# A causal convolution folded into its projection's weights, and the gates' products moved one stage later

## The chip, the cores and the metric

The kernel runs on one core of one Trainium2 chip. The metric is device time in microseconds (us) from the start to the end of one execution; the kernel before was run three times, and its median is given. A core has five engines that work side by side: TensorE multiplies matrices (PE in the profile, PEld for its weight loads), VectorE (DVE) and ScalarE (ACT) work element by element, GpSimd (POOL) too, and SyncE (SP) issues the DMAs here. Each takes its instructions in order.

## The reference

The input x is 16 images of 256 channels and 32x32 points. Layer 0 is x + attention block(group norm(x)). Layer 1, with which the change deals, is a Mamba-like layer: for each image, with L = 1024 tokens,

```python
xs = group_norm(x) as tokens + (rel_h + rel_w)              # (L, 256)
ctx = sigmoid(conv1d(xs, gate_w, 3 taps, pad 1) + gate_b)   # the gates, (L, 256)
u, z = split(xs @ in_proj_w.T)                              # (L, 512) each
uc[l] = conv_b + sum over t in 0..3 of conv_w[:, t] * u[l - 3 + t]   # each channel alone, causal
u = silu(uc)
dt, Bm, Cm = split(u @ x_proj_w.T)                          # 16, 64, 64
delta = softplus(dt @ dt_proj_w.T + dt_proj_b)              # (L, 512)
h[l] = exp(delta[l] * A) * h[l - 1] + delta[l] * u[l] * Bm[l]   # 512 x 64 states
y[l] = h[l] . Cm[l] + u[l] * D
out = x + ((y * silu(z)) @ out_proj_w.T) * ctx
```

All of it is fp32, but for delta's pieces, which are held as three bf16 parts.

## The kernel before, in words

**The scan.** Images ("batches", b) are done one after the other. The state recurrence of a batch is cut into 256 units (b, t, k, q, i): 2 halves of the tokens, 4 blocks of 128 channels, 4 quarters, 8 pairs of channels. A unit handles 2 x 64 states on 128 partitions and 512 tokens, twice (e = 0, 1). `load` fetches delta*u spread over the partitions (tile dub, L832), `inputs` multiplies it by B on GpSimd (L842), `decay` multiplies a selection matrix by delta's pieces on TensorE (L851) and takes exp on ScalarE (L854), `scan` runs the recurrence on VectorE (L864), and `outputs` sums h*C over the states on TensorE, in bursts of 64 passes (L901), copies (L909) and turns (L913).

**The side work.** Beside batch b's scans, a Python generator issues what batch b+1 needs, and what batch b-1 has still to do: `first_norm`, `gate_and_store` (of b-1), `attention_layer`, and `scan_inputs`, in this order. Each `yield` names the cost of the step just issued. The main loop deals the steps over the units at an even rate:

```python
total = steps * len(parts)        # steps: sum of the yields of one preparation
...
total += GATE
...
rate, due = total / (UNITS - AHEAD - 3), 0.0
```

so that a change of any yield changes how many units each stage is spread over. In a unit n the order is load(n+6), inputs(n+4), scan(n), decay(n+2), then the side steps that have come due, then a step of `outputs`. On TensorE, ScalarE, VectorE and GpSimd the program order is kept as written; SyncE's DMAs may be placed otherwise. Batch 0's preparation runs alone, ahead of the first scan, and beside the last batch only `gate_and_store` runs.

**The stages of `scan_inputs`.** In order: group norm (into xp, with room for one zero on each side), the position added, the z stage (L580, L585, L569), the u stage, the x stage (L667, L671), softplus (L686 to L733). In the u stage `project(d, hf)` multiplies a half (512 tokens) of block d by its weights, two products of 128 rows each (L601), copies it to `up` (L606) and starts `u` with the last tap and the bias (L607). `tap(d, t)` adds one of the other three taps on VectorE over 1024 tokens (L615). Then tanh (L652) and u = (tanh + 1) * u (L655) make the silu. `gate(o, hf, q)` makes a quarter of the gates' block o: six products of 256 columns and one for the bias (L630, L634), and after every second one a tanh (L636). Gates are interleaved with the taps. Each step of a u block costs 1.6, four of them, and the first two projections 1 each.

**Buffers.** Tiles of 1024 columns come from the pool `wide` (10 buffers), weights of a stage from one tile of 4672 columns, matrix products from the pool mm (2 banks of PSUM) beside the scan; the pool accp is one bank, used by attention. `decay` has 4 banks, two units' worth.

Of the kernel before, what the change touches and what calls it, by code (L numbers as in the profile page):

```python
# [11 lines left out]
F32 = mybir.dt.float32  # L12
BF16 = mybir.dt.bfloat16
AF = mybir.ActivationFunctionType
ALU = mybir.AluOpType
# [4 lines left out]
P = 128  # L20
C = 256
KC = C // P
L = 1024
HL = 512
# [4 lines left out]
DI = 512  # L29
ND = DI // P  # L30
NS = 64
RANK = 16
CONV = 4
# [19 lines left out]
def attention_then_scan_kernel(  # L53
# [18 lines left out]
    nc = tc.nc  # L72
    B = x.shape[0]

    def pool(name, bufs, **kw):
        return ctx.enter_context(tc.tile_pool(name=name, bufs=bufs, **kw))

    const = pool("const", 1)
    wts = pool("wts", 1)
    wide = pool("wide", 10)  # L80
    half = pool("half", 4)
    ptp = pool("ptp", 4)
    small = pool("small", 2)
# [4 lines left out]
    dram1 = pool("dram1", 1, space=DRAM)  # L88
# [9 lines left out]
    def psum(name, dims=P):  # L98
        src = mm if beside["scan"] else next(alone)
        return src.tile([P, HL], F32, name=name, tag="mm" if src is mm else "a")[:dims]  # L100

    def work(name, n=L):
        return wide.tile([P, L + 2 + CONV], F32, name=name, tag="wide")[:, :n]

    def hwork(name):
        return half.tile([P, HL], F32, name=name, tag="half")

    def hs(h):
        return ts(h, HL)
# [67 lines left out]
    t = work("ones_s")[:1]  # L177
# [9 lines left out]
        nc.sync.dma_start(rel[ts(k, P), :], t)  # L187


    def weights(*specs):  # L190
        w = wts.tile([P, 4672], F32, name="w", tag="w")
        at, views, fetches = 0, [], []
        for src, k in specs:
            n = src.shape[-1]
            if k == 0:
                v = w[: src.shape[0], at : at + n]
                at += n
            else:
                v = w[:, at : at + k * n].rearrange("p (k e) -> p k e", k=k)
                src = src.rearrange("(k p) e -> p k e", p=P)  # L200
                at += k * n
            views.append(v)
            fetches.append(partial(nc.sync.dma_start, v, src))
        return views, fetches
# [102 lines left out]
    def fetch(to, src, k):  # L307
        t = work("xs")
        nc.sync.dma_start(t, src[ts(k, P), :])  # L309
        to.append(t)  # L310
# [226 lines left out]
    def scan_inputs(b):  # L537
        st = state[b]
        (win_s, wg_s, wx_s, wdt_s), bring = weights(
            (w_in, KC), (w_gate.rearrange("c t o -> c (t o)"), KC), (w_x, ND), (w_dt, 0)  # L540
        )
        wg_s = wg_s.rearrange("p k (t o) -> p k t o", t=3)
        xs = st.pop("xs")
        xp = [work("xp", L + 2) for _ in range(KC)]
        body = [t[:, 1 : L + 1] for t in xp]
        for t in xp:
            nc.vector.memset(t[:, 0:1], 0.0)
            nc.vector.memset(t[:, L + 1 : L + 2], 0.0)
        rels = []
        yield from along(  # L550
            group_norm(xs, body),
            [partial(nc.sync.dma_start, st["xr"][ts(k, P), :], xs[k]) for k in range(KC)]
# [14 lines left out]
        def finish_z():  # L567
            for d, hf, z, t, ps in ready:
                nc.vector.scalar_tensor_tensor(z[:, hs(hf)], t, 1.0, ps, ALU.add, ALU.mult)  # L569
                if hf == 1:  # L570
                    nc.sync.dma_start(zs[ts(d, P), :], z)
            ready.clear()

        for d in range(ND):
            z = work("z")
            for hf in range(2):
                finish_z()
                ps = psum("z_ps")
                for k in range(KC):
                    nc.tensor.matmul(  # L580
                        ps, win_s[:, k, ds(DI + d * P, P)], body[k][:, hs(hf)],
                        start=(k == 0), stop=(k == KC - 1),
                    )
                t = hwork("z_t")
                nc.scalar.activation(t, ps, AF.Tanh, scale=0.5)  # L585
                ready.append((d, hf, z, t, ps))
                yield 1
        del z, t, ps

        us, ups = [], []  # L590
        ud = dram.tile([DI, L], F32, name="ud", tag="ud")
        gs = dram.tile([C, L], F32, name="gs", tag="gs")

        def project(d, hf):
            if hf == 0:
                ups.append(work("up", L + CONV - 1))
                nc.vector.memset(ups[d][:, : CONV - 1], 0.0)
                us.append(work("u"))
            ps = psum("u_ps")
            for k in range(KC):  # L600
                nc.tensor.matmul(  # L601
                    ps, win_s[:, k, ts(d, P)], body[k][:, hs(hf)],
                    start=(k == 0), stop=(k == KC - 1),
                )
            last = d * CONV + CONV - 1
            nc.scalar.copy(ups[d][:, ds(CONV - 1 + hf * HL, HL)], ps)  # L606
            nc.scalar.activation(  # L607
                us[d][:, hs(hf)], ps, AF.Identity,
                bias=cbh[:, d : d + 1], scale=cwh[:, last : last + 1],
            )  # L610

        def tap(d, t):
            i = d * CONV + t
            u = us[d]
            nc.vector.scalar_tensor_tensor(  # L615
                u, ups[d][:, t : t + L], cwh[:, i : i + 1], u, ALU.mult, ALU.add
            )

        gates = {}

        def gate(o, hf, q):
            if (hf, q) == (0, 0):
                gates["g"] = work("g")
            if q == 0:
                gates["ps"] = psum("g_ps")
            g, ps = gates["g"], gates["ps"]
            first = o * HL + hf * 2 + q
            for i in range(3 * KC):
                k, t = divmod(i, 3)
                nc.tensor.matmul(  # L630
                    ps[:, ts(q, C)], xp[k][:, ds(first + t, P, 4)], wg_s[:, k, t, :],
                    start=(i == 0), stop=False,
                )
            nc.tensor.matmul(ps[:, ts(q, C)], one_row, gate_b, start=False, stop=True)  # L634
            if q == 1:
                nc.scalar.activation(g[:, hs(hf)], ps, AF.Tanh, scale=0.5)  # L636
                if hf == 1:
                    nc.sync.dma_start(gs[ts(o, P), :], g)

        finish_z()  # L640
        project(0, 0)
        yield 1
        project(0, 1)
        yield 1
        for d in range(ND):
            for t in range(2):
                tap(d, t)
                if d + 1 < ND:
                    project(d + 1, t)
                yield 1.6  # L650
            tap(d, 2)
            nc.scalar.activation(ups[d][:, :L], us[d], AF.Tanh)  # L652
            gate(d // 2, d % 2, 0)
            yield 1.6
            nc.vector.scalar_tensor_tensor(us[d], ups[d][:, :L], 1.0, us[d], ALU.add, ALU.mult)  # L655
            ups[d] = None
            nc.sync.dma_start(ud[ts(d, P), :], us[d])
            gate(d // 2, d % 2, 1)
            yield 1.6
        gates.clear()  # L660
        del xp, body
        dt, bc = work("dt"), work("bc")
        for hf in range(2):
            for dst, lo, n in ((dt, 0, RANK), (bc, RANK, 2 * NS)):
# [38 lines left out]
        yield 1  # L703
        for d in range(ND):
            items = [more(d, *items[0]), begin(d, 1)]
            yield 1
            items[1] = more(d, *items[1])
            rest(*items[0])
            yield 1.4
            rest(*items[1])  # L710
            for ps, e, s in items:
                nc.scalar.activation(s, s, AF.Ln)
            yield 1.7
            pc = [ptp.tile([P, L], BF16, name="pc", tag="pt") for _ in range(3)]
            for hf, (ps, e, s) in enumerate(items):
                nc.vector.tensor_tensor(ps, s, ps, ALU.subtract)
                nc.scalar.copy(pc[0][:, hs(hf)], ps)
            yield 1.4
            du = work("du")
            for hf, (ps, e, s) in enumerate(items):  # L720
                nc.vector.tensor_tensor(du[:, hs(hf)], us[d][:, hs(hf)], ps, ALU.mult)
            nc.sync.dma_start(duv[d], du.rearrange("d (t c) -> d t c", t=NT))
            yield 1.4
            for hf, (ps, e, s) in enumerate(items):
                nc.vector.tensor_tensor(ps, ps, pc[0][:, hs(hf)], ALU.subtract)
                nc.scalar.copy(pc[1][:, hs(hf)], ps)
            yield 1.4
            for hf, (ps, e, s) in enumerate(items):
                nc.vector.tensor_tensor(pc[2][:, hs(hf)], ps, pc[1][:, hs(hf)], ALU.subtract)
            items, ps, e, s = [], None, None, None  # L730
            for p in range(3):
                for e in range(2):
                    nc.sync.dma_start(dpv[d, p, e], pc[p][e:P:2])  # L733
            if d + 1 < ND:
                items = [begin(d + 1, 0)]
            yield 1.4
        st.update(zs=zs, gs=gs, ud=ud, rows=rows, dps=dps, dus=dus)
        st["ys"] = dram.tile([DI, L], F32, name="ys", tag="ys")
        yield 1
# [321 lines left out]
```

## Time and profile before

| what | us |
|---|---|
| median of 3 runs (13815.34 to 13842.49) | 13833.62 |
| the profiled execution, whole | 13784.86 |
| its span, first to last instruction | 13782.7 |
| start of the first scan | 392.9 |
| one batch of 256 units, seven batches in | 849.4 |
| last batch (only `gate_and_store` beside it) | 676.7 |
| VectorE busy, all | 12135.5 |
| TensorE busy, all | 11113.2 |
| GpSimd busy, all | 10477.2 |
| taps L615, all 192 | 300.9 |

Durations below come from the profiled execution, and comparisons of whole times are made from the median. A group's line reads: source line, engine, operation, output<-inputs, shapes, count | busy us, mean ns of one | idle time of the engine ahead of it, and what ended that. The granted TensorE clock (PEclk) is a share of full speed.

### The profile page before, as it was taken

To read this page: it belongs to the slowest core of one execution; us is meant where nothing else is said; L and a number is where in the kernel's file an instruction comes from. 1 tells how busy PE (TensorE), PEld (TensorE's weight loads), DVE (VectorE), ACT (ScalarE), POOL (GpSimd) and SP (SyncE) were. 2 spreads that over 40 slices of the span, in tenths; PEclk is the share of its full clock that TensorE was granted. 3 is DMA by queue.
4 is the path that set the end of the run, shared out by engine and by line. 5 is a ranking of instruction groups with operands and counts; after the bars stand their busy time and mean duration, and the time that the engine had idled before them with its cause. 6 is when DMAs were issued, how large, how long until landed. Compare 5 with 4: busy or idle time off the path is not lost. (4 is left out here: it accounts for less than half of the span.)

```text
span 13782.7 us, 435036 instructions
## 1 busy us (share of the span) xinstructions
PE 11113.2 (81%) x185744; PEld 5728.7 (42%) x185744; DVE 12135.5 (88%) x11699; ACT 8088.7 (59%) x14245; POOL 10477.2 (76%) x8214
## 2 busy tenths in 40 slices
PE   7787878878787787978879788797887978878767
PEld 3344444444444444444444444444444444434434
DVE  3898898898898889888898888889888898888898
ACT  3666665656655565655656655566555655556644
POOL 0787777777787777777777787777777777777788
PEclk8686767867777686876767777677776776867767
DMA  1566566565665656556565565656656565565666
GB/s 55 196 207 230 187 214 208 201 222 196 211 207 199 218 201 223 194 199 218 197 231 186 197 226 191 232 185 202 219 191 230 187 214 205 194 228 187 209 219 223
DMA packets 964174, 2804.18 MB, mean 203 GB/s; under 512 B 138162, under 2 KB 285747, under 8 KB 962228
## 3 DMA queue, kind: packets, MB, share of 16 engines
q1 hardware_dynamic: 962228, 2776.34, 58.8%
q8 instruction: 1452, 23.79, 0.7%
q14 instruction: 494, 4.05, 0.1%
HBM read 2514.18 MB, written 261.62 MB: 201 GB/s over the span
## 5 line engine op out<-in xcount | busy, mean ns | idle before, releaser
L842 POOL TENSOR_TENSOR dub<-dub,bt 128x512 f32<-128x512 f32 x8192 | 10422.4, 1307 | 3254.5 <-DMA dub<-dus 2878.4
L854 ACT ACTIVATE a<-a,acol 128x512 f32<-128x512 f32 x8192 | 5064.9, 660 | 3728.2 <-PE a L851 3689.1
L864 DVE TENSOR_TENSOR_SCAN h<-a,last,dub 128x512 f32<-128x512 f32 x4096 | 4932.9, 1261 | 227.0 <-POOL dub L842 128.8
L864 DVE TENSOR_TENSOR_SCAN h<-a,dub 128x512 f32<-128x512 f32 x4096 | 4700.9, 1201 | 276.7 <-POOL dub L842 186.6
L851 PE MATMUL a<-pieces,pick 48*128 48x512 bf16 x8192 | 2914.9, 480 | 2103.1 <-DVE h L864 2037.8
L901 PEld LDWEIGHTS yb<-h,cd 128*32 128x32 f32 x131072 | 2677.2, 140 | 2166.2 <-issue 1847.3
L901 PE MATMUL yb<-h,cd 128*32 128x64 f32 x131072 | 3090.5, 265 | 160.9 <-DVE yb L891 115.9
L851 PEld LDWEIGHTS <-pick 48*128 48x128 bf16 x8192 | 498.0, 96 | 2507.4 <-issue 2293.2
L408 PE MATMUL s_ps<-ka,qa 32*128 32x512 f32 x2048 | 1115.7, 1009 | 23.2 <-DVE mx L399 15.2
L399 DVE TENSOR_REDUCE mx<-s_ps 128x1 f32<-128x512 f32 x1024 | 654.9, 678 | 279.0 <-PE s_ps L408 278.2
L913 PEld LDWEIGHTS yb<-turn,y 128*16 128x16 f32 x32768 | 418.9, 120 | 960.3 <-ACT y L909 484.6
L909 ACT COPY y<-yb 128x256 f32<-128x256 f32 x1024 | 383.4, 374 | 693.6 <-PE yb L901 688.3
L913 PE MATMUL yb<-turn,y 128*16 128x32 f32 x32768 | 555.2, 216 | 193.8 <-ACT y L909 173.0
L444 PE MATMUL st_ps<-qa,ka 33*128 33x512 f32 x2048 | 590.2, 613 | 25.9 <-ACT pt L452 25.5
L432 PE MATMUL av<-pt,vv 128*64 128x512 f32 x2048 | 572.7, 635 | 4.3 <-ACT sums L390 3.3
L452 ACT ACTIVATE pt<-st_ps 128x512 f32<-128x512 f32 x1024 | 558.9, 609 | 28.8 <-PE st_ps L444 28.4
L408 PEld LDWEIGHTS s_ps<-ka,qa 32*128 32x128 f32 x2048 | 345.4, 274 | 402.3 <-DVE mx L399 221.4
L630 PE MATMUL g_ps<-w,xp 128*128 128x256 f32 x1536 | 475.2, 468 | 0.0
L630 PEld LDWEIGHTS g_ps<-w,xp 128*128 128x128 f32 x1536 | 401.9, 329 | 137.6 <-issue 92.6
L789 PE MATMUL m_ps<-w,xs 128*128 128x256 f32 x1024 | 316.7, 459 | 10.9 <-DVE xs L764 10.9
L921 ACT COPY yo<-yb 128x256 f32<-128x256 f32 x512 | 193.1, 377 | 222.2 <-PE yb L913 219.7
L615 DVE SCALAR_TENSOR_TENSOR u<-up,cwh,u 128x1024 f32<-128x1024 f32 x192 | 300.9, 1567 | 23.8 <-ACT u L607 23.6
(135 smaller groups left out, 7593.8 us busy)
## 6 DMA issues: line engine op xcount, KB each, us to landing
dub<-dus SPq DMA_DIRECT2D x4096, 512.0 KB
dps<-pc SPq DMA_DIRECT2D x384, 128.0 KB
pieces<-dps SPq DMA_DIRECT2D x1024, 48.0 KB
xs<-in_x_dram SPq DMA_DIRECT2D x64, 512.0 KB
xs<-kept SPq DMA_DIRECT2D x64, 512.0 KB
zs<-z SPq DMA_DIRECT2D x64, 512.0 KB
ud<-u SPq DMA_DIRECT2D x64, 512.0 KB
dus<-du SPq DMA_DIRECT2D x64, 512.0 KB
```

Source lines behind the costliest of these rows:

```text
L399: nc.vector.tensor_reduce(mx[:, e, c, hf : hf + 1], s, AX.X, ALU.max)
L408: nc.tensor.matmul(s, qa[r, ts(c, P)], ka[r, hs(hf)], start=True, stop=True)
L432: nc.tensor.matmul(av[ts(e, 2 * DH)], vv[j // (NJ // 2)][:, j % (NJ // 2), 2 * pair + e, :], pts[e], start=(j == 0), stop=(j == NJ - 1),)
L444: nc.tensor.matmul(s, ka[r, ts(j, P)], qa[r, hs(hf)], start=True, stop=True)
L452: nc.scalar.activation(pt, s, AF.Exp)
L630: nc.tensor.matmul(ps[:, ts(q, C)], xp[k][:, ds(first + t, P, 4)], wg_s[:, k, t, :], start=(i == 0), stop=False,)
L842: nc.gpsimd.tensor_tensor(v, v, blocks[b, t]["bt"], ALU.mult)
L851: nc.tensor.matmul(a, w, pieces[r], start=True, stop=True)
L854: nc.scalar.activation(a, a, AF.Exp, scale=acol[:, at : at + 1])
L864: nc.vector.tensor_tensor_scan(now["h", q % 2][:, 2 * i + e, :], decays[n][e], loaded[n][:, e, :], first, ALU.mult, ALU.add,)
L901: nc.tensor.matmul(yb[ts(g, 32), ts(s, 64)], cd[:, at // 16, ts(c, 32)], hbuf[:, :, at : at + 4], start=(c == 0), stop=(c == 3),)
L913: nc.tensor.matmul(out4[32 * s : 32 * s + 16, half, e], y2[:, 64 * s + e : 64 * s + 64 : 4], turn[:, e], start=True, stop=True,)
```

## The change

The convolution's taps go into the weights: conv_w[e, t] * in_proj_w[e, c] is a weight matrix for each tap t, and u of a block is the sum over 2 halves of the channels and 4 taps of one product each, with the tokens shifted by t, all summed in PSUM. These weights are computed once, ahead of everything, on GpSimd, and kept in DRAM (wcv, 512 KB for each of 4 blocks); each batch fetches them, block by block. xp has three zeros ahead and one behind. ScalarE takes tanh of the sum into SBUF and adds the bias in place, and VectorE makes the silu in halves, one step later (`finish_u`). The calls of `gate` move from the u stage into softplus, two for each d, with their sums in accp's bank. Only z's half of w_in is fetched among the weights. The yields change: the u stage's sum goes from 27.6 to 17.2, softplus' from 39.8 to 42.6. The diff, cut to its core:

```diff
-    wide = pool("wide", 10)
+    wide = pool("wide", 11)
...
+    wcv = dram1.tile([ND * P, KC * CONV * P], F32, name="wcv", tag="wcv")
+    taps = dram1.tile([ND * CONV, P], F32, name="taps", tag="taps")
+    ps = psum("taps_ps", ND * CONV)[:, :P]
+    nc.tensor.matmul(ps, cwh, ident, start=True, stop=True)
+    t = work("taps_s", P)[: ND * CONV]
+    nc.scalar.copy(t, ps)
+    nc.sync.dma_start(taps, t)
+    wu = work("wu").rearrange("p (k e) -> p k e", k=KC)
+    nc.sync.dma_start(wu, w_in[:, :DI].rearrange("(k p) e -> p k e", p=P))
+    for d in range(ND):
+        if d % 2 == 0:
+            row = work("row")
+            nc.sync.dma_start(
+                row,
+                taps[ds(d * CONV, 2 * CONV)].rearrange("i e -> (i e)").partition_broadcast(P),
+            )
+        t = work("wcs").rearrange("p (k t e) -> p k t e", k=KC, t=CONV)
+        for k in range(KC):
+            nc.gpsimd.tensor_tensor(
+                t[:, k], row[:, ts(d % 2, CONV * P)].rearrange("p (t e) -> p t e", t=CONV),
+                wu[:, k, ts(d, P)].unsqueeze(1).to_broadcast([P, CONV, P]), ALU.mult,
+            )
+        nc.sync.dma_start(wcv[ts(d, P), :], t.rearrange("p k t e -> p (k t e)"))
...
-            (w_in, KC), (w_gate.rearrange("c t o -> c (t o)"), KC), (w_x, ND), (w_dt, 0)
+            (w_in[:, DI:], KC), (w_gate.rearrange("c t o -> c (t o)"), KC), (w_x, ND), (w_dt, 0)
...
-        xp = [work("xp", L + 2) for _ in range(KC)]
-        body = [t[:, 1 : L + 1] for t in xp]
+        xp = [work("xp", L + CONV) for _ in range(KC)]
+        body = [t[:, CONV - 1 : CONV - 1 + L] for t in xp]
...
+        def finish_u():
+            for d, hf, t, ps in ready:
+                nc.vector.scalar_tensor_tensor(us[d][:, hs(hf)], t, 1.0, ps, ALU.add, ALU.mult)
+                if hf == 1:
+                    nc.sync.dma_start(ud[ts(d, P), :], us[d])
+            ready.clear()
...
         def project(d, hf):
             if hf == 0:
-                ups.append(work("up", L + CONV - 1))
-                nc.vector.memset(ups[d][:, : CONV - 1], 0.0)
                 us.append(work("u"))
+            w = wcs[d].rearrange("p (k t e) -> p k t e", k=KC, t=CONV)
             ps = psum("u_ps")
-            for k in range(KC):
+            for i in range(KC * CONV):
+                k, t = divmod(i, CONV)
                 nc.tensor.matmul(
-                    ps, win_s[:, k, ts(d, P)], body[k][:, hs(hf)],
-                    start=(k == 0), stop=(k == KC - 1),
+                    ps, w[:, k, t], xp[k][:, ds(hf * HL + t, HL)],
+                    start=(i == 0), stop=(i == KC * CONV - 1),
                 )
-            last = d * CONV + CONV - 1
-            nc.scalar.copy(ups[d][:, ds(CONV - 1 + hf * HL, HL)], ps)
-            nc.scalar.activation(
-                us[d][:, hs(hf)], ps, AF.Identity,
-                bias=cbh[:, d : d + 1], scale=cwh[:, last : last + 1],
-            )
-
-        def tap(d, t):
-            i = d * CONV + t
-            u = us[d]
-            nc.vector.scalar_tensor_tensor(
-                u, ups[d][:, t : t + L], cwh[:, i : i + 1], u, ALU.mult, ALU.add
-            )
+            t = hwork("u_t")
+            nc.scalar.activation(t, ps, AF.Tanh, bias=cbh[:, d : d + 1])
+            nc.scalar.activation(ps, ps, AF.Identity, bias=cbh[:, d : d + 1])
+            ready.append((d, hf, t, ps))
...
-                gates["ps"] = psum("g_ps")
+                gates["ps"] = accp.tile([P, HL], F32, name="g_ps", tag="av")
...
+        fetch(wcs, wcv, 0)
         finish_z()
-        project(0, 0)
-        yield 1
-        project(0, 1)
         yield 1
         for d in range(ND):
-            for t in range(2):
-                tap(d, t)
-                if d + 1 < ND:
-                    project(d + 1, t)
-                yield 1.6
-            tap(d, 2)
-            nc.scalar.activation(ups[d][:, :L], us[d], AF.Tanh)
-            gate(d // 2, d % 2, 0)
-            yield 1.6
-            nc.vector.scalar_tensor_tensor(us[d], ups[d][:, :L], 1.0, us[d], ALU.add, ALU.mult)
-            ups[d] = None
-            nc.sync.dma_start(ud[ts(d, P), :], us[d])
-            gate(d // 2, d % 2, 1)
-            yield 1.6
-        gates.clear()
-        del xp, body
+            for hf in range(2):
+                if hf == 0 and d + 1 < ND:
+                    fetch(wcs, wcv, d + 1)
+                finish_u()
+                project(d, hf)
+                yield 1.9
+            wcs[d] = None
+        finish_u()
+        yield 1
...
             items = [more(d, *items[0]), begin(d, 1)]
-            yield 1
+            gate(d // 2, d % 2, 0)
+            yield 1.4
             items[1] = more(d, *items[1])
...
                 nc.vector.tensor_tensor(ps, ps, pc[0][:, hs(hf)], ALU.subtract)
                 nc.scalar.copy(pc[1][:, hs(hf)], ps)
-            yield 1.4
+            gate(d // 2, d % 2, 1)
+            yield 1.7
```

Left out of it: the smaller weight tile (3648 columns for 4672), the zeros at xp's ends, the index of z's weights, the first column of `gate`'s tokens (moved by the two more zeros), and the release of us[d], the gates' tile and xp at the end of softplus.

More of the change, by code (lines that the diff above doesn't have):

```diff
@@ L187, in attention_then_scan_kernel @@
         nc.sync.dma_start(rel[ts(k, P), :], t)
+    wcv = dram1.tile([ND * P, KC * CONV * P], F32, name="wcv", tag="wcv")
[21 more added lines that the diff above has]
+        nc.sync.dma_start(wcv[ts(d, P), :], t.rearrange("p k t e -> p (k t e)"))
+    del wu, row, t, ps
     def weights(*specs):
-        w = wts.tile([P, 4672], F32, name="w", tag="w")
+        w = wts.tile([P, 3648], F32, name="w", tag="w")
         at, views, fetches = 0, [], []
@@ L543, in scan_inputs @@
         xs = st.pop("xs")
-        xp = [work("xp", L + 2) for _ in range(KC)]
-        body = [t[:, 1 : L + 1] for t in xp]
+        xp = [work("xp", L + CONV) for _ in range(KC)]
+        body = [t[:, CONV - 1 : CONV - 1 + L] for t in xp]
         for t in xp:
-            nc.vector.memset(t[:, 0:1], 0.0)
-            nc.vector.memset(t[:, L + 1 : L + 2], 0.0)
-        rels = []
+            nc.vector.memset(t[:, : CONV - 1], 0.0)
+            nc.vector.memset(t[:, L + CONV - 1 :], 0.0)
+        rels, wcs = [], []
         yield from along(
@@ L580, in scan_inputs @@
                     nc.tensor.matmul(
-                        ps, win_s[:, k, ds(DI + d * P, P)], body[k][:, hs(hf)],
+                        ps, win_s[:, k, ts(d, P)], body[k][:, hs(hf)],
                         start=(k == 0), stop=(k == KC - 1),
@@ L588, in scan_inputs @@
         del z, t, ps
-        us, ups = [], []
+        us = []
         ud = dram.tile([DI, L], F32, name="ud", tag="ud")
         gs = dram.tile([C, L], F32, name="gs", tag="gs")
+        def finish_u():
[4 more added lines that the diff above has]
+            ready.clear()
         def project(d, hf):
             if hf == 0:
-                ups.append(work("up", L + CONV - 1))
-                nc.vector.memset(ups[d][:, : CONV - 1], 0.0)
                 us.append(work("u"))
+            w = wcs[d].rearrange("p (k t e) -> p k t e", k=KC, t=CONV)
             ps = psum("u_ps")
-            for k in range(KC):
+            for i in range(KC * CONV):
+                k, t = divmod(i, CONV)
                 nc.tensor.matmul(
-                    ps, win_s[:, k, ts(d, P)], body[k][:, hs(hf)],
-                    start=(k == 0), stop=(k == KC - 1),
-                )
-            last = d * CONV + CONV - 1
-            nc.scalar.copy(ups[d][:, ds(CONV - 1 + hf * HL, HL)], ps)
-            nc.scalar.activation(
-                us[d][:, hs(hf)], ps, AF.Identity,
-                bias=cbh[:, d : d + 1], scale=cwh[:, last : last + 1],
-            )
-        def tap(d, t):
-            i = d * CONV + t
-            u = us[d]
-            nc.vector.scalar_tensor_tensor(
-                u, ups[d][:, t : t + L], cwh[:, i : i + 1], u, ALU.mult, ALU.add
-            )
+                    ps, w[:, k, t], xp[k][:, ds(hf * HL + t, HL)],
+                    start=(i == 0), stop=(i == KC * CONV - 1),
+                )
+            t = hwork("u_t")
+            nc.scalar.activation(t, ps, AF.Tanh, bias=cbh[:, d : d + 1])
+            nc.scalar.activation(ps, ps, AF.Identity, bias=cbh[:, d : d + 1])
+            ready.append((d, hf, t, ps))
         gates = {}
@@ L624, in gate @@
             if q == 0:
-                gates["ps"] = psum("g_ps")
+                gates["ps"] = accp.tile([P, HL], F32, name="g_ps", tag="av")
             g, ps = gates["g"], gates["ps"]
-            first = o * HL + hf * 2 + q
+            first = o * HL + hf * 2 + q + CONV - 2
             for i in range(3 * KC):
@@ L721, in scan_inputs @@
                 nc.vector.tensor_tensor(du[:, hs(hf)], us[d][:, hs(hf)], ps, ALU.mult)
+            us[d] = None
             nc.sync.dma_start(duv[d], du.rearrange("d (t c) -> d t c", t=NT))
@@ L736, in scan_inputs @@
             yield 1.4
+        gates.clear()
+        del xp, body
         st.update(zs=zs, gs=gs, ud=ud, rows=rows, dps=dps, dus=dus)
```

## The prediction, on record before the result

> **What bounds the kernel now.** I read the page's busy shares first, then its groups, then windows cut at the stages of one batch, then the instructions of the tile u_ps. Busy time, share, instructions:
>
> ```profile
> PE 11113.2 (81%) x185744; PEld 5728.7 (42%) x185744; DVE 12135.5 (88%) x11699; ACT 8088.7 (59%) x14245; POOL 10477.2 (76%) x8214
> ```
>
> No engine is at 100%, so the limit changes by stage. Next, seven batches in, one row each for the attention scores, the rest of attention and the second norm, z, u, x and softplus (columns: length, then busy time of each engine with its instructions, clock, DMA):
>
> ```profile
> core 0: us, PE busy (x) PEld busy (x) DVE busy (x) ACT busy (x) POOL busy (x), PEclk, DMA share, GB/s
> 5590.14:5872.04 281.90, 263.78 (x4448) 122.82 (x4446) 250.75 (x254) 179.88 (x338) 226.94 (x184) 0.79 0.56 189
> ...
> 6012.87:6101.27 88.40, 77.28 (x1153) 49.00 (x1152) 82.68 (x71) 48.13 (x81) 75.88 (x52) 0.90 0.58 193
> 6101.27:6120.90 19.63, 19.63 (x270) 8.13 (x268) 12.50 (x11) 9.74 (x18) 14.13 (x12) 1.00 0.58 186
> 6120.90:6236.07 115.17, 82.81 (x1486) 40.74 (x1488) 109.88 (x117) 87.48 (x147) 81.18 (x67) 0.54 0.63 212
> ```
>
> The u stage (88.40) and softplus (115.17) are bound by VectorE, 94 and 95% busy. The x stage is bound by TensorE, busy all of it, with VectorE at 64%. The stages that the change touches sit on both sides. The same windows counted for scans alone show how many scan units (two scans each) run in a stage, first in this batch (u, softplus), then in the side work of batch 0 (scores, u, softplus), which spreads the same steps thinner, over more units:
>
> ```profile
> 6012.87:6101.27 88.40, 60.49 (x50) 0.90 0.58 193
> ...
> 6120.90:6236.07 115.17, 82.02 (x69) 0.54 0.63 212
> ```
>
> ```profile
> 501.22:795.20 293.98, 234.84 (x205) 0.79 0.58 197
> ...
> 940.37:1032.07 91.70, 65.66 (x55) 0.91 0.63 208
> ...
> 1050.80:1174.58 123.78, 89.39 (x75) 0.54 0.63 212
> ```
>
> Three more scan units in softplus cost 8.6 us (2.6 to 2.9 each). Ten more in the scores (205 against 185 scans) cost 12.1 us (1.2 each), since TensorE limits there. Last, the operations in dispute:
>
> ```profile
> L615 DVE SCALAR_TENSOR_TENSOR u<-up,cwh,u 128x1024 f32<-128x1024 f32 x192 | 300.9, 1567 | 23.8 <-ACT u L607 23.6
> ...
> L601 PE MATMUL u_ps<-xp,w 128*128 128x512 f32 x512 | 253.6, 619 | 0.0
> ```
>
> ```profile
> 6016.88 1.26 DVE L864 TENSOR_TENSOR_SCAN h<-a,last,dub 128x512 f32<-128x512 f32 x1
> ...
> 6018.06 1.10 PE L901 MATMUL yb<-h,cd 128*32 128x64 f32 x64
> ...
> 6019.10 0.39 PE L851 MATMUL a<-pieces,pick 48*128 48x512 bf16 x2
> ...
> 6019.41 1.99 PE L601 MATMUL u_ps<-xp,w 128*128 128x512 f32 x4
> ```
>
> There are 512 records of u_ps where the code has 256 products: an fp32 product is two passes. Passes start 0.428 us apart (6019.95, 6020.38 are starts of their weight loads), so a product is 0.86 us. A unit's scan work on TensorE is one burst of outputs (1.10, or 0.47 or none; 5.3 in eight units) and the decays (0.45 with their gap): 1.1 us at full clock. The x stage tests this: 16 products of 0.86 and 5.5 units of 1.1 are 19.8, the row says 19.63.
>
> **What the skill says.** The Trainium skill, "TensorE: Matmul & The Clock Gate", Part 1, has the clock at half or full by recent activity; the trace agrees: mean 0.54 in softplus, 1.00 in the dense x stage. The same page, "Step-by-step: what each phase is for", says matmuls stay in program order: a decay behind a long product waits, as the timeline's order shows. "SBUF — State Buffer", "SBUF: two separate sides", says that a VectorE operation with two SBUF inputs and a GpSimd one exclude each other; the taps agree, at 1.25 us least, 1.57 mean and 2.37 most. The new product of u has one input in PSUM, as z's has.
>
> **The change, part by part, per batch.**
> *Dealing of units.* From the yields one batch costs 281.3 (254.7 and 26.6), dealt over 247 units at 1.139 each. The u stage's yields fall from 27.6 to 17.2, softplus' rise from 39.8 to 42.6: 273.7, or 1.108 a unit. So u takes 15.5 units where the table shows 25; softplus takes 37.3 for 34.5; the rest some 6 more. All 256 units remain, so those lost in u are run elsewhere.
> *u stage.* VectorE loses 12 taps of 1.567 = 18.8 us and the 10 units of scans; u's last product stays (4 of 1.476 before, 8 of about 0.68 after, as z's line L569 at 681 ns). ScalarE loses one copy of two, no limit. TensorE gains 6 products for each of 8 halves, 48 x 0.86 = 41 us, and loses the gates. New sum: a half is 16 passes, 1.9 for the first four as shown and 12 x 0.428, 7.05 us; eight are 56.4; with 15.5 units of 1.1 (17) and about 1.5 at the ends, 75 us. VectorE needs only 15.5 x 2.45 + 5.5 = 43, so TensorE becomes the bound. 75 for 88.4: **-13.4**.
> *Softplus.* 37.3 units are what batch 0's row shows (75 scans): 123.8 for 115.2, **+8.6**, without gates.
> *Gates, moved here.* Eight bursts of 14 passes. In the u stage they last 3.8 us at full clock and 5.0 to 5.9 where the clock was half; here it is 0.54, so 5.4. Behind the burst on TensorE stand an output burst (1.1 to 2) and the decays of three units on, then ScalarE's exp (0.66) and the scan. These come about 8.4 us after the decay ahead of the burst, 10 where d_ps (0.99 a record, two records) stands in front. VectorE has two units of scans (4.9) and 2 to 3 us of softplus work meanwhile. Wait: 0 to 1 us and 2 to 3; but part meets ScalarE waits already there. Bounds 0 and 18 (all cold); I take **+8**. ScalarE's tanh of g (0.60, four times) and the two stores of g move too; SP then waits for g behind softplus' own stores, covered by dub's six units of lead.
> *Rest.* Scores: 2.6 units of 1.2, 3.1; the remainder of attention and the second norm 1.5, by the rise from 113.3 to 118.4 us for three units; head of the batch 1.3 units of 2.4, 3: **+7.6**, bounds 5 and 10.
> *DMA.* Four fetches of 512 KB, half of w_in (512 KB) less: 1.5 MB in 847 us, about 1% of 203 GB/s. The first fetch has about a unit until TensorE needs it; if late, scans already decayed cover some 5 us. I cost it at nothing, up to 3 if that cover is gone.
> *Sum:* -13.4 + 8.6 + 8 + 7.6 = **+10.8** a batch, in 15 batches (the last has no such stages): +162.
> *Once.* Before the scans, the u stage runs alone in 43.2 us with TensorE busy for all of it; it needs 56.4 and 1, so +14. Gates there meet a TensorE that is busy 10.9 of 51.3 us: +3. Building the weights (PE, ACT, two reads back, eight GpSimd products of about 1.3 us, stores) overlaps x's first loads in part: 0 to 20, I take 8. Together +25.
> Total +187 on the profiled execution (13784.86, its span 13782.7): 13972. That execution lies 49 below the median of the runs, 13833.62; the same +187 there gives **14020**, 1.35% slower.
>
> **Rivals.**
> (1) *VectorE stays the bound in u* (faster). If a unit of u needs under about 45 us of TensorE in all, a pass below 0.25 us, the stage falls to VectorE's 43: -45 + 8.6 + 8 + 7.6 = -21, x15 + 25 = -287: 13547. For it: VectorE is the busiest engine by share. Against: 128 passes of 0.428 already make 55. The change of sign comes at a u stage of about 62 us, everything else held.
> (2) *Gates are hidden and units elsewhere cheap.* Gates 0, softplus +6, rest +6: -1.4, x15 + 25 = about 0: 13838. For it: the gates cost almost nothing in u now. Against: the clock and d_ps in front.
> (3) *Gates stall every scan behind them.* +18 for gates, +10 for rest, u at 80: -8.4 + 8.6 + 18 + 10 = +28, x15 + 35: 14290. For it: clock 0.54. Against: a burst raises the clock by itself.
> That the change doesn't do what it says is not among them: its yields and products are plain in the code.
>
> **Chances.** Forecast 0.58 (own range 13900 to 14190), rival 1 0.13, rival 2 0.15, rival 3 0.14. About 0.2% is what a measurement of this kernel can tell from no change. Of rival 2 a third each falls faster, same and slower; a little of the forecast's lower end (0.02) is the same: faster 0.18, same 0.07, slower 0.75. The range leaves out rival 1 and the top of rival 3: 13780 to 14270.
>
> **What would show it.** In the changed profile: L615's taps gone, DVE about 300 us less in total, PE's u_ps with 2048 records in 128 groups of some 7 us; a u stage of some 75 us with about 31 scans, PE busy all through, VectorE near 60%; a softplus stage of 125 to 135 us with waits of h for a before some scans after gates; the span before the first scan some 25 us longer than 393. I am wrong if the u stage is under 62 us or TensorE idles in it, if units moved elsewhere cost under 1 us, or if softplus stays at 124 with the gates in it.

## The result, and the profile after

| | before | after |
|---|---|---|
| median, us (4 runs each) | 13838.06 | 14176.13 |
| ratio, 95% interval | | 1.0243 (1.0224 to 1.0261) |
| profiled execution, span | 13782.7 | 14173.2 |
| one batch, mean of 14 | 847.3 | 870.7 |
| start of the first scan | 392.9 | 434.2 |

The change makes the kernel 2.4% slower: 338 us by the medians, 390 by the two profiled spans, which the sums below use; the profiled execution of the kernel before lies 53 us below its median, so these sums can be some 3 us a batch too high. The forecast was 187 us, with the right sign and inside its range, but only about half of what came. First the busy shares:

```profile
PE 11604.7 (82%) x187282; PEld 5964.6 (42%) x187282; DVE 11852.0 (84%) x11507; ACT 8015.3 (57%) x14182; POOL 10329.7 (73%) x8222
```

VectorE lost 283 us of work and TensorE's busy time grew by 492; every engine but TensorE has a smaller share of a longer span. The windows of the stages, seven batches in (scores, u, x, softplus; columns as in the prediction):

```profile
core 0: us, PE busy (x) PEld busy (x) DVE busy (x) ACT busy (x) POOL busy (x), PEclk, DMA share, GB/s
...
5782.56:6073.86 291.30, 267.27 (x4484) 125.19 (x4482) 257.99 (x260) 182.62 (x342) 235.97 (x191) 0.79 0.57 188
...
6216.14:6289.71 73.57, 72.56 (x732) 33.86 (x732) 35.65 (x33) 24.94 (x45) 37.66 (x32) 0.96 0.45 161
6289.71:6311.72 22.01, 21.38 (x335) 9.06 (x333) 17.46 (x15) 11.99 (x22) 15.82 (x13) 1.00 0.51 172
6311.72:6444.28 132.56, 99.50 (x1575) 61.84 (x1574) 115.60 (x121) 92.12 (x155) 88.72 (x72) 0.74 0.61 199
```

Counted for scans alone, u and softplus:

```profile
6216.14:6289.71 73.57, 31.05 (x26) 0.96 0.45 161
6311.72:6444.28 132.56, 87.47 (x73) 0.74 0.61 199
```

The u stage has changed sides: TensorE is busy for all but 1 us of its 73.57, VectorE for half (it was 94%). Softplus has four scans more and VectorE waits 17 us in it, where it waited 5. And the scores, which the diff does not touch, are some 10 us longer, with three scan units more. The groups of the new products and of u's last steps (the helper that fetches the weights names its tile xs):

```profile
L635 PE MATMUL u_ps<-xp,xs 128*128 128x512 f32 x2048 | 950.0, 619 | 34.4 <-DMA xs<-wcv 34.4
...
L623 DVE SCALAR_TENSOR_TENSOR u<-u_t,u_ps 128x512 f32<-128x512 f32 x128 | 88.1, 688 | 609.2 <-ACT u_ps L641 609.2
...
L640 ACT ACTIVATE u_t<-u_ps,cbh 128x512 f32<-128x512 f32 x128 | 88.0, 688 | 782.3 <-PE u_ps L635 782.3
```

VectorE is idle for 609 us ahead of L623: it waits for ScalarE, which waits for TensorE's bursts (782 us ahead of L640). The first new product waits for its weights, 34 us in 16 batches.

All stages, mean of the 14 batches that have all of them beside them (each from its first instruction to that of the next, the tail from softplus' last piece to the next batch's first scan; scan units in brackets):

| stage | before | after | difference |
|---|---|---|---|
| head (first norm, the other batch's gate_and_store, attention's start) | 171.5 (49.5) | 173.6 (50.6) | +2.1 |
| scores | 283.0 (92.3) | 292.7 (95.2) | +9.7 |
| attention's end, MLP | 54.1 (15.0) | 52.5 (15.0) | -1.6 |
| norm, position | 58.2 (16.4) | 60.0 (17.4) | +1.8 |
| z | 28.2 (6.7) | 30.8 (8.9) | +2.6 |
| u | 88.9 (24.9) | 73.4 (12.8) | -15.5 |
| x | 19.6 (5.4) | 22.0 (7.0) | +2.4 |
| softplus | 115.2 (33.9) | 133.9 (36.3) | +18.7 |
| tail | 28.5 (12.0) | 31.8 (13.0) | +3.3 |
| sum | 847.3 | 870.7 | +23.4 |

Fourteen such batches are +327; batch 0, with less side work, +16, the part ahead of the scans +41, the last batch and the end +6: 390 in all.

Of the 41, 19 come from building the weights. The timeline of the changed kernel's first 42 us:

```profile
24.91 9.79 POOL L208 TENSOR_TENSOR wcs<-row,wu 128x512 f32<-128x512 f32 x8 [23.60 <-DMA row<-taps]
27.41 7.63 SPq L212 DMA_DIRECT2D wcv<-wcs  x4
35.10 1.25 SPq L335 DMA_DIRECT2D xs<-in_x_dram  x2
...
39.94 2.52 DVE L254 TENSOR_REDUCE gn_s<-xs 128x16 f32<-128x1024 f32 x2 [22.15 <-DMA xs<-in_x_dram]
```

The loads of x (35.10) stand on SyncE behind the stores of the new weights, which wait for GpSimd's products; before, they were issued at 14 and 18 us. The first norm starts 22 us later, and only 3 of these are made up before the scores. The rest of the 41: 14 in u, 4 in z (the lead step and the first fetch), 5 in softplus.

### The profile page after: what moved, and what is told of

Read it like the earlier page. It is cut to its first block, busy times and chain, and to the rows that moved or that the text cites. A ratio compares the mean times of both kernels' runs of the same rounds, so it can differ in the third digit from the quotient of the medians.

```text
span 14173.2 us, 437924 instructions
## 1 busy us (share of the span) xinstructions
PE 11604.7 (82%) x187282; PEld 5964.6 (42%) x187282; DVE 11852.0 (84%) x11507; ACT 8015.3 (57%) x14182; POOL 10329.7 (73%) x8222
## 5 line engine op out<-in xcount | busy, mean ns | idle before, releaser
L863 POOL TENSOR_TENSOR dub<-dub,bt 128x512 f32<-128x512 f32 x8192 | 10264.9, 1284 | 3768.0 <-DMA dub<-dus 3350.5
L872 PE MATMUL a<-pieces,pick 48*128 48x512 bf16 x8192 | 2813.7, 468 | 2088.4 <-DVE h L885 2049.3
L922 PEld LDWEIGHTS yb<-h,cd 128*32 128x32 f32 x131072 | 2579.7, 136 | 2047.1 <-issue 1668.2
L922 PE MATMUL yb<-h,cd 128*32 128x64 f32 x131072 | 2977.4, 260 | 140.1 <-DVE yb L912 110.3
L635 PE MATMUL u_ps<-xp,xs 128*128 128x512 f32 x2048 | 950.0, 619 | 34.4 <-DMA xs<-wcv 34.4
L635 PEld LDWEIGHTS u_ps<-xp,xs 128*128 128x128 f32 x2048 | 393.0, 197 | 540.6 <-issue 487.9
L623 DVE SCALAR_TENSOR_TENSOR u<-u_t,u_ps 128x512 f32<-128x512 f32 x128 | 88.1, 688 | 609.2 <-ACT u_ps L641 609.2
L655 PE MATMUL g_ps<-w,xp 128*128 128x256 f32 x1536 | 572.4, 545 | 8.2 <-ACT g L661 8.2
L478 ACT ACTIVATE pt<-st_ps 128x512 f32<-128x512 f32 x1024 | 558.1, 608 | 28.4 <-PE st_ps L470 27.4
L655 PEld LDWEIGHTS g_ps<-w,xp 128*128 128x128 f32 x1536 | 450.3, 329 | 213.5 <-issue 119.9
L640 ACT ACTIVATE u_t<-u_ps,cbh 128x512 f32<-128x512 f32 x128 | 88.0, 688 | 782.3 <-PE u_ps L635 782.3
```

The lines of the kernel that those rows point to most:

```text
L635: nc.tensor.matmul(ps, w[:, k, t], xp[k][:, ds(hf * HL + t, HL)], start=(i == 0), stop=(i == KC * CONV - 1),)
L655: nc.tensor.matmul(ps[:, ts(q, C)], xp[k][:, ds(first + t, P, 4)], wg_s[:, k, t, :], start=(i == 0), stop=False,)
L863: nc.gpsimd.tensor_tensor(v, v, blocks[b, t]["bt"], ALU.mult)
L872: nc.tensor.matmul(a, w, pieces[r], start=True, stop=True)
L922: nc.tensor.matmul(yb[ts(g, 32), ts(s, 64)], cd[:, at // 16, ts(c, 32)], hbuf[:, :, at : at + 4], start=(c == 0), stop=(c == 3),)
```

## The experiments

Twelve kernels; their ratios are to runs of the kernel before on the same chip. Stages are given with their mean or median over those 14 batches. Edits are cut to their core.

**1. What do the gates cost in softplus?** The changed kernel without the gates' six products; only the bias goes through the tanh, so this kernel computes something else.

```diff
-            for i in range(3 * KC):
-                k, t = divmod(i, 3)
-                nc.tensor.matmul(
-                    ps[:, ts(q, C)], xp[k][:, ds(first + t, P, 4)], wg_s[:, k, t, :],
...
-            nc.tensor.matmul(ps[:, ts(q, C)], one_row, gate_b, start=False, stop=True)
+            nc.tensor.matmul(ps[:, ts(q, C)], one_row, gate_b, start=True, stop=True)
```

> The changed kernel with the gates' six products left out (the bias alone goes through the tanh), so it is not the reference's result. Theory A (bursts of gates delay the decays behind them in softplus, some 13 us a batch): softplus falls from 133.9 to about 121, all other stages stay, the part before the first scan some 6 shorter; 13975 us in all. Theory B (gates are hidden in softplus, and its 18.7 us more are its added scan units): 14150 to 14176.

Measured: 14075.9 us, 1.0184 (1.0156 to 1.0212).

```profile
6284.19:6409.99 125.80, 91.67 (x1580) 47.53 (x1579) 115.24 (x121) 93.97 (x158) 86.85 (x71) 0.56 0.64 210
```

Softplus falls to 125.8, 8.1 less; VectorE's work is the same 115 us. Of softplus' 18.7 the gates' products are thus 8.1; the other 10.6 are the added units and what is left of the gates (tanh, bias, stores), which number 4 takes apart. Theory A holds, but its size of 13 was too large: I had put all of VectorE's added waiting on the gates. The time is 100 us above theory A's: some 70 of them for the smaller gain, and in this kernel's profile the part ahead of the scans was also 20 us longer and not 6 shorter (last section).

**2. The gates moved alone, in the kernel before.**

```diff
-            gate(d // 2, d % 2, 0)
             yield 1.6
...
-            gate(d // 2, d % 2, 1)
             yield 1.6
...
             items = [more(d, *items[0]), begin(d, 1)]
+            gate(d // 2, d % 2, 0)
             yield 1
...
                 nc.scalar.copy(pc[1][:, hs(hf)], ps)
+            gate(d // 2, d % 2, 1)
             yield 1.4
```

> The kernel before with its gates moved to softplus (sums in the third pool's bank, the same yields); the taps stay on VectorE. Theory A (gates cost their wait in softplus, nothing is won in u, where VectorE is the bound): u 87 for 89, softplus 127 to 129 for 115, the part before the first scan some 15 shorter; 14000 us, 1.2% slower than before. Theory B (gates are hidden in softplus): 13810 to 13830, not slower than before.

Measured: 13955.2 us, 1.0102 (1.0080 to 1.0124). Softplus 128.2 for 115.2, u 84.1 for 88.9, x 21.4 for 19.6: +12.3 a batch. Theory A, 45 us below its estimate: moving the gates out of a stage that VectorE bounds wins 5 and costs 13.

**3. Should u just be spread over more units?**

```diff
-                yield 1.9
+                yield 4.5
```

> The changed kernel with the yield of each half of u at 4.5 for 1.9: u is spread over some 32 units, all other stages over fewer. Theory A (a scan unit costs 1.1 us in the u stage, where TensorE is the bound, and about 2.1 elsewhere): u 93 us for 73, softplus 129, all else some 30 us a batch shorter; 13950 us. Theory B (the 41 us of TensorE work that a batch gained are what counts, wherever the units run): 14150 to 14200.

Measured: 14511.9 us, 1.0508 (1.0483 to 1.0533). Theory A fell, and so did B, which expected no change: all other stages shrank (scores 280.6, softplus 128.2), by 36 us together, but u took 129.5 us for its 31 units, where theory A's sum for TensorE was 93. The timelines of VectorE, TensorE and ScalarE in it:

```profile
6389.33 4.81 DVE L885 TENSOR_TENSOR_SCAN h<-a,last,dub 128x512 f32<-128x512 f32 x4 [6.06 <-POOL dub L863]
6394.06 0.66 DVE L623 SCALAR_TENSOR_TENSOR u<-u_t,u_ps 128x512 f32<-128x512 f32 x1
6394.63 4.80 DVE L885 TENSOR_TENSOR_SCAN h<-a,last,dub 128x512 f32<-128x512 f32 x4
6406.01 4.81 DVE L885 TENSOR_TENSOR_SCAN h<-a,last,dub 128x512 f32<-128x512 f32 x4 [6.58 <-issue]
```

```profile
6394.71 9.37 PE L635 MATMUL u_ps<-xp,xs 128*128 128x512 f32 x16
6404.01 0.39 PE L872 MATMUL a<-pieces,pick 48*128 48x512 bf16 x2
```

```profile
6404.11 0.69 ACT L640 ACTIVATE u_t<-u_ps,cbh 128x512 f32<-128x512 f32 x1 [8.06 <-PE u_ps L635]
6404.70 0.65 ACT L641 ACTIVATE u_ps<-u_ps,cbh 128x512 f32<-128x512 f32 x1
6405.27 2.39 ACT L875 ACTIVATE a<-a,acol 128x512 f32<-128x512 f32 x4
```

A burst of 16 passes starts at 6394.71. VectorE then has four scans (two units), whose decays are done, and is through at 6399.4. The next decay comes after the burst, at 6404.01, and its exp on ScalarE after the tanh and the bias of that burst: the next scan starts at 6406.01. The wait is 6.58 us; over the eight bursts of this window such waits come to 51. The trace puts four of the eight down to GpSimd's dub, as at 6389.33; there too the first exp behind the burst had ended only 0.1 us before. The burst is 9.4 us, not 7.05: the granted clock is 0.50 in its first 3.4 us and 0.90 in the rest. So the reading is that the limit is not a sum, but the length of a burst against the scans decayed ahead, 4.9 us; number 5 tests it.

**4. The gates back in u, beside the new products.**

```diff
                 project(d, hf)
+                gate(d // 2, d % 2, hf)
                 yield 1.9
...
-            gate(d // 2, d % 2, 0)
             yield 1.4
...
-            gate(d // 2, d % 2, 1)
             yield 1.7
```

> The changed kernel with its gates back in the u stage, one call beside each half of u, the yields as in the changed kernel. Theory A (TensorE is the bound of u, so gates add all of their time there; softplus is freed of their wait): u 104 us for 73, softplus 121 for 134; 14440 to 14460 us. Theory B (u has room on TensorE): 13980.

Measured: 14415.6 us, 1.0435 (1.0407 to 1.0464); u 100.1, softplus 123.2. Theory A, 24 us below its span: in the new u stage TensorE has no room, and the gates cost 27 us there, against 11 in softplus. With no gates in it at all, and the units of the changed kernel, softplus is 8.0 above the kernel before: so its 18.7 are 8.0 for the added units and 10.7 for the gates, 8.1 of them the products.

**5 to 7. Is it the length of a burst?** Number 5 is number 3 with each half in four steps (part p issues products 2p and 2p + 1), number 6 the changed kernel with the gates' calls halved, number 7 has both.

```diff
-                project(d, hf)
-                yield 4.5
+                for part in range(4):
+                    project(d, hf, part)
+                    yield 1.125
```

> As the kernel with u spread (4.5 for each half), but each half's eight products are issued in four steps of two, 1.125 each; the sum of yields, the products and all other stages are the same. Theory A (while TensorE works on one burst, VectorE has just the two units of scans whose decays are done, 4.9 us; a longer burst leaves it idle): u takes 93 to 98 us for 129.5, the rest as before, 14000 us. Theory B (so many scan units beside so much TensorE work cost 129 us whatever the size of a burst): 14500.

Measured: 14135.3 us, 1.0233 (1.0217 to 1.0248). The u stage, first in number 3, then in this kernel:

```profile
6349.17:6478.87 129.70, 109.98 (x1407) 50.47 (x1406) 78.69 (x71) 50.71 (x90) 77.58 (x64) 0.82 0.49 160
```

```profile
6189.81:6298.64 108.83, 97.93 (x1407) 44.30 (x1406) 79.00 (x71) 51.18 (x90) 78.61 (x65) 0.95 0.57 196
```

It is 107.1 in the median, 22 us less than number 3 with the same products, units and yields, and VectorE stands still for 30 us of it instead of 51. That is theory A's way, though not down to its 93 to 98; TensorE is 90% busy, and the time is 135 us above A's. Two things changed together: TensorE is idle for 10.9 us instead of 19.7, and its busy time is 97.9 instead of 110.0, at a mean clock of 0.95 for 0.82. The shorter bursts brought both; no run shows what the waits alone would have given at an equal clock.

Number 6, against the changed kernel (part 0 is the first three products, part 1 the rest):

```diff
-            gate(d // 2, d % 2, 0)
             yield 1.4
...
             rest(*items[0])
+            gate(d // 2, d % 2, 0, 0)
...
                 nc.scalar.copy(pc[0][:, hs(hf)], ps)
+            gate(d // 2, d % 2, 0, 1)
...
             nc.sync.dma_start(duv[d], du.rearrange("d (t c) -> d t c", t=NT))
+            gate(d // 2, d % 2, 1, 0)
...
-            gate(d // 2, d % 2, 1)
+            gate(d // 2, d % 2, 1, 1)
```

> The changed kernel with each call of the gates cut in two (three products, then three and the bias), put on four of softplus' seven steps, away from the two that hold d_ps; the yields are the same. Theory A (a burst waits only where it outlasts two units of scans): softplus falls from 133.9 to about 126, where it was without the gates' products; 14060 to 14080 us. Theory B (the gates' time on TensorE counts, not the length of a burst): 14160 to 14180.

Measured: 14110.5 us, 1.0211 (1.0190 to 1.0231). Softplus 127.6 for 133.9: most of what the gates' products cost there is gone, with the same passes. Theory B is out. But two things were changed for theory A: the bursts are halved, and they no longer stand right behind d_ps. The traces of the changed kernel and of number 1 say which bursts made VectorE wait: with each idle stretch of VectorE in softplus counted to the burst last begun (up to 14 us back), the four bursts that follow d_ps have 14.9 us a batch (9.4 without the products), the other four 2.3 (none). So some 5.5 of the 8 us come from bursts with d_ps in front. How much halving alone would win is not shown. The time is 31 us above A's span; the part ahead of the scans was 18 us longer in this kernel's profile (last section).

> Both splits together: u spread in steps of two products, gates in halves. Theory A: u 93 to 98, softplus 120 to 122 for 128, 13880 to 13900 us, near the kernel before. Theory B: 14500.

Measured: 14058.6 us, 1.0169 (1.0150 to 1.0187). Softplus 118.1, u 107.2; 860.9 a batch. Theory B's 14500 is out, but the time is 159 us above theory A's span, mostly for u's size. This is the best form of the change that was found, and it is still 1.7% slower than before.

**8. Why are the scores longer?** An empty step, which brings the rate of dealing back to that of before:

```diff
         st["ys"] = dram.tile([DI, L], F32, name="ys", tag="ys")
         yield 1
+        yield 7.6
```

> The changed kernel with an empty step of 7.6 at the end of a batch's side work: the sum of yields is again 281.3, so all stages ahead of it are spread as in the kernel before. Theory A (the scores stage cost 9.7 us more because its steps were spread over 3 more units): scores 283 us for 293, the parts around it back too, the tail some 14 longer; 14180 to 14230 us. Theory B (something else of the change, the shared bank or the buffers, slows the scores): scores stay at 291 to 293, 14330 us.

Measured: 14295.1 us, 1.0348 (1.0328 to 1.0369). Scores and tail:

```profile
5850.72:6133.16 282.44, 267.58 (x4446) 124.73 (x4444) 250.59 (x252) 178.30 (x334) 225.94 (x183) 0.77 0.58 187
...
6512.22:6558.38 46.16, 33.19 (x841) 18.27 (x840) 45.34 (x39) 27.40 (x48) 37.73 (x32) 0.70 0.76 255
```

The scores are back at 283 (median 283.5), the tail is 14 longer: theory A for both. But softplus took 138.8 for 133.9 (136.9 in the mean) at nearly the same units, which neither theory has; the time, of two runs only, is 65 us above A's span.

**9. Is it TensorE that bounds u?** Two of the four taps left out, so this kernel computes something else:

```diff
-            for i in range(KC * CONV):
-                k, t = divmod(i, CONV)
+            for i in range(KC * 2):
+                k, t = i // 2, 2 + i % 2
```

> The changed kernel with two of the four taps left out of u's sums (four products for each half instead of eight), so it is not the reference's result. Theory A (TensorE is the bound of u): a half is 3.6 us of products, u 45 to 48 us for 73, nothing else moves; 13740 to 13780 us. Theory B (u takes 73 us for its waits and units, not for its products): 14150 to 14176.

Measured: 13764.7 us, 0.9963 (0.9948 to 0.9978).

```profile
6032.62:6079.39 46.77, 45.26 (x669) 21.57 (x669) 34.87 (x33) 25.07 (x45) 33.81 (x29) 0.95 0.65 232
```

u is 46.8 for 73.6: four products of 0.86 taken from each of eight halves are 27.4, and 26.8 are gone. Nothing else in a batch moved. Theory A. It is the only variant with products in place of taps that is faster than before, by 0.4%, and it does half of the convolution.

**10 to 12. Does a cheap place for scan units pay?** The kernel before, with x's yields at 2.9 (number 10), then at 2.2 (number 11); in number 12 x is as it was, and an empty step stands at the end.

```diff
                 nc.scalar.copy(dst[:n, hs(hf)], ps)
-                yield 1.6
+                yield 2.9
```

```diff
         st["ys"] = dram.tile([DI, L], F32, name="ys", tag="ys")
         yield 1
+        yield 2.4
```

> The kernel before, nothing of the change in it, with the yields of the x stage's four steps at 2.9 for 1.6. Theory A (a scan unit costs 1.1 us of time where TensorE is the bound and about 2.2 elsewhere, so units belong beside TensorE's work as long as bursts stay under 4.9 us): x 25 us over 10 units for 19.6 over 5.4, all else 11 a batch shorter; 13740 to 13770 us, 0.5% faster than before. Theory B (a unit costs the same anywhere): within 0.1% of before.

Measured: 13840.5 us, 1.0011 (1.0002 to 1.0021). Theory A fails: x 26.8 over 10.4 units, but no gain elsewhere to pay for it.

> The same with 2.2 for 1.6. Theory A: x 22.3 us over 7.5 units, 0.2 to 0.3% faster than before. Theory B: within 0.1% of before.

Measured: 13711.5 us, 0.9921 (0.9906 to 0.9937), three times what A allows.

> The kernel before with an empty step of 2.4 at the end of a batch's side work and x's yields as they were: the rate of dealing is that of the kernel with x at 2.2 (1.149 a unit), but the units freed go to the tail. Theory A (x's extra units, beside TensorE's work, won the 0.8%): x 19.6, head about 166, tail 33, no faster than before, 13800 to 13840 us. Theory B (how the steps fall against the pattern of outputs at that rate won it, mostly in the head and attention's end): head 166 to 167, o to f 50, tail 33; 13750 to 13780 us, still faster than before.

Measured: 13719.2 us, 0.9922 (0.9909 to 0.9934). Head, and attention's end:

```profile
5395.57:5563.05 167.48, 122.43 (x2147) 73.77 (x2146) 144.91 (x138) 87.89 (x157) 140.79 (x108) 0.67 0.72 245
...
5849.34:5898.88 49.54, 38.72 (x637) 16.87 (x638) 46.00 (x46) 28.71 (x48) 39.88 (x33) 0.81 0.52 168
```

Theory B, and 31 us below its span: a step that does nothing makes the kernel 0.8% faster, as much as number 11 by the medians. Head 167.0 for 171.5 with 1.1 units less, attention's end 49.7 for 54.1 with the same 15 units, against a tail of 32.8 for 28.5. The rate rose by 0.9%, from 1.139 to 1.149, and with it the way in which steps and units fall together. In the profiles number 11 gains 8.5 us a batch and number 12 6.0; the 2.5 between them are of the size that theory A gave number 11, and no run separates them from other effects of the dealing. Numbers 11 and 12 are the fastest kernels of this study; neither has anything of the change in it.

## Why the prediction was right or wrong

*The u stage* (-13.4): right in its mechanism. It took 73.4 us for the predicted 75, bound by TensorE; number 9 shows the price of a product (26.8 for 27.4). It lost more units than I counted (12.1, not 9.5), since the two steps of 1 at its ends fall to z and x in the profile. With the 12.8 units that it has, my sum gives 72, and the wait for weights brings it to 74: so that 75 was met so closely is in part luck. z, u and x together give -10.5.

*Softplus' units* (+8.6): right; with no gates in softplus it is +8.0 (number 4).

*The gates* (+8): right for the products, 8.1 (number 1); with tanh, bias and stores it is 10.7 (number 4), inside the bounds of 0 and 18. The mechanism is the one given, waits behind bursts, longer where d_ps stands in front: halved bursts away from d_ps win 6.3 back (number 6).

*Rest* (+7.6, bounds 5 and 10): this is the term that failed. Scores, the remainder, head, tail, z and x came to +20.3. The scores, priced at 3.1, measured 9.7; z, x and the tail, which took some 5 units more and were not in the sum, 8.3; the others 2.3, where 4.5 was set. In the scores the failed reading is that of batch 0's row as a price: "2.6 units of 1.2" took a line through two points, 92 and 102 units, but the stage is no line. Over 88.5 (number 3), 92.3 and 95.2 units it measures 280.6, 283.0 and 292.7 us. Number 8 shows that it is the rate that costs this, not the shared bank or the buffers; number 12 shows that the rate alone, with no work moved, is worth 0.8%, or 6.0 us a batch by the profiles. So a unit has no fixed price, and the term's bounds should have been some 6 us wider each way; the 20.3 lies outside even those, because z, x and the tail were left out of the sum.

*Once* (+25): 41. The u part was right (+14). Building the weights, taken at 8 in bounds of 0 to 20, was 19: almost nothing overlapped, as SyncE's queue put x's loads behind it.

*DMA* (nothing, up to 3): the fetch of the first block is not covered; TensorE waits about 2 us a batch for it, inside the bound.

The sum with the measured terms is 15 x 22.9 + 41 and 6 at the end, the 390 of the profiles. Rival 1 (VectorE stays the bound) is excluded by the u stage's row and number 9; its point of decision was placed too high. At the measured rest, u must fall to about 47 us to break even (73.4 less 390 / 15), not 62, and there number 9 sits, just faster. Rival 3's total, 14290, is 114 us above what came and the forecast's, 14020, 156 below, but rival 3 has the wrong terms: the gates cost 8 to 11, not 18, and u is 73, not 80. Rival 2 (gates hidden, no change) is excluded by the time and by number 1.

Two things stay open: which waits make the scores, the head and attention's end depend on the rate, and why softplus took 3 to 5 us more in number 8. Both were measured, not explained; no kernel here takes the pattern of outputs apart, so that pattern is a guess.

## What to carry to other kernels

Moving work from the busiest engine to the second busiest is paid for by the stage: here 19 us a batch of VectorE's taps became 48 more products, 41 us of TensorE, in a stage where TensorE had 11 us left. Where a feeder runs a fixed number of units ahead of a scan, work on the feeder is better put in short bursts (here those units last 4.9 us, and a burst of products 7 to 9.4); the same products in quarters took 22 us less. And where a schedule deals out steps by costs, try an empty step first: if that moves the time by 0.8%, differences of that size between two versions say nothing yet about the work that was changed.

## What the runs showed of the hardware that was not expected

The part ahead of the scans, alone on the core, has two lengths in its scores: 152 to 155 us in the profiles of before, after and numbers 2, 9, 10 and 12, 177 in those of numbers 1, 3 to 8 and 11, with identical work. The mean granted clock in it goes with the length: 0.79 to 0.82 in the first group, 0.67 to 0.68 in the second. The 22 us between them are 0.16% of a run, which a comparison of profiles from different groups contains. Number 8 and the changed kernel have the same instructions there and fall into different groups, so it is not the work; what it is stays open.

The mean granted clock of a stage is also not told by TensorE's busy share. In softplus that share is 72% before, 75% after and 73% without the gates' products (number 1), and the clock is 0.54, 0.74 and 0.56. It rose where the gates' products were put in, in bursts of 14 passes (3.8 to 6.0 us) as well as in bursts of six and eight (number 6, 0.77); that is as far as these runs show.
